# Softplus in one ScalarE function, earlier use of PSUM banks, and sums of states that add to a seeded bank, in a Mamba and attention kernel

## The chip, the cores and the metric

The kernel runs on one core of a Trainium2 chip. The core has five engines with queues of their own: TensorE (PE; PEld is its weight load), VectorE (DVE), ScalarE (ACT), GpSimd (POOL) and SyncE (SP), which here issues nearly all transfers. The metric is the device time of one execution in microseconds (us).

## What is computed

Eight images of 384 channels by 1024 positions go through two layers. The first normalizes, runs a Mamba block forwards and backwards over the 1024 positions, and adds a 3x3 depthwise convolution with a gate. The second is causal attention with six heads, and a feed-forward with binarized weights and quantized activations, which by the reference's grouping works on the first five of the eight images. Cut to what the change touches:

```python
def mamba(x, in_proj_w, conv1d_w, conv1d_b, x_proj_w, dt_proj_w, dt_proj_b, A_log, D_param, out_proj_w):
    ...
    dt, Bm, Cm = jnp.split(x_dbl, [dt_rank, dt_rank + D_STATE], axis=-1)
    delta = jax.nn.softplus(jnp.einsum('blr,dr->bld', dt, dt_proj_w) + dt_proj_b)
    A = -jnp.exp(A_log)
    deltaA = jnp.exp(delta[..., None] * A)
    deltaBu = (delta * u)[..., None] * Bm[:, :, None, :]
    def step(h, inp):
        dA, dBu, c = inp
        h = dA * h + dBu
        return (h, jnp.einsum('bdn,bn->bd', h, c))
    ...
    y = ys.transpose(1, 0, 2) + u * D_param
    y = y * silu(z)
    return jnp.einsum('bld,od->blo', y, out_proj_w)
```

There are 16 states for each of the 384 channels, two directions, and all is float32.

## The kernel before

**Who sets the order.** The program first records every operation (`Plan.record`) with a rank, its place in the order of recording. `Plan.place` then plays the whole kernel through with a cost for each operation, gives every engine the ready operation of lowest rank whose buffers are free, and places its tiles; `Plan.emit` issues all in that order. An engine's queue is therefore fixed when the program is built. `hurry(offset=...)` lowers the rank of what is recorded in it; `together()` makes one operation of several instructions on one engine. All of them reach the profile as line 364, so groups of instructions are told apart by their tiles.

**The scans.** An image has four parts (direction and half of the positions, `PARTS`), three blocks of 128 channels, four groups of states and two halves of channels: 96 units of work, 768 in all. For one unit POOL multiplies delta u by B (`s_first`, two units ahead); ACT makes exp(delta A) in one of two PSUM banks ("da") and DVE scans, twice (`s_scan`, 512 positions each); POOL multiplies by C. There are six buffers for the products (tile `scan_g`). For every second unit `s_sum` sums the states of a pair with four matmuls (tile `ps_y`, one bank); four pairs make one part of one channel block. `s_gate` then closes it: the first direction's y plus D u is kept in `yt`; in the second direction three VectorE steps make y + D u, add yt and multiply by z. `slots` records the scan steps with a rank 600 lower than their place.

**The rest.** `before_scan` prepares an image: norm, input projection, convolutions, u, B, C and delta. `delta` makes softplus for 128 channels and 512 positions from `dp`, a PSUM bank that a matmul with `const_wdt` fills. It takes exp(-|x|), 1 + that, its logarithm, adds max(x, 0) and corrects the rounding of 1 + e: five ScalarE steps and three VectorE steps, before DVE multiplies by u and ACT copies delta to SBUF. Both are stored to DRAM, from where the scans load them spread over partitions. There are 12 such deltas for an image, 96 in all. `attention` is the second layer for one image, `feed_forward` its second half; five PSUM banks ("any") serve all of this. `spread_over` interleaves lists of such steps by their share of their total cost; `before_scan` of images 3 to 7 is interleaved with the feed-forward of images 0 to 4 in this way. Images 0 to 2 are prepared and the weights binarized in an opening stage. At the end `due` times spread the scan slots over the rest, and the attention of the last image's second half runs alone.

ScalarE keeps one table of functions loaded; the kernel stays with the one that has Exp and Ln (`LOG_EXP`), and loads another for Silu, Tanh and Gelu in blocks that end with `preload_act_table_set(LOG_EXP)`.

Of the kernel before, what the change touches and what calls it, by code (L numbers as in the profile page):

```python
# [13 lines left out]
ALU = mybir.AluOpType  # L14
# [146 lines left out]
class Plan:  # L161
# [84 lines left out]
    def place(self):  # L246
# [47 lines left out]
        while events:  # L294
            now = events[0][0]
            while events and events[0][0] <= now:
                heapq.heappop(events)
            moved = True
            while moved:
                moved = False  # L300
                for e in engines:
                    while waiting[e] and waiting[e][0][0] <= now:
                        op = heapq.heappop(waiting[e])[2]
                        if op.start is None:
                            heapq.heappush(ready[e], (op.rank, next(count), op))
                    while free_at[e] <= now and ready[e]:
                        aside, op, held = [], None, set()
                        while ready[e]:
                            item = heapq.heappop(ready[e])
                            if item[2].start is not None:  # L310
                                continue
                            if fits(item[2], now, held):
                                op = item[2]
                                break
                            aside.append(item)
                        for item in aside:
                            heapq.heappush(ready[e], item)
                        if op is None:
                            break
                        op.name, op.start, moved = e, now, True  # L320
                        for t in op.tiles:
                            if t.place is None:
                                k = t.kind
                                k.free.sort()
                                t.place = k.free.pop(0)[1]
                        if op.dma:
                            free_at[e] = now + 0.06
                            dma_free = max(dma_free, now + 1.2) + op.time
                            op.end = dma_free + 1.2
                        else:  # L330
                            op.end = free_at[e] = now + op.time
                        heapq.heappush(events, (free_at[e], next(count), e))
                        done.append(op)
                        for t in op.tiles:
                            users_left[id(t)] -= 1
                            if not users_left[id(t)]:
                                at = max(u.end for u in t.users) + self.SIGNAL
                                t.kind.free.append((at, t.place))
                                t.kind.freed += 1
                                heapq.heappush(events, (at, next(count), e))  # L340
                        for nxt in op.behind:
                            nxt.left -= 1
                            if not nxt.left:
                                release(nxt)
# [33 lines left out]
def kernel(  # L378
# [104 lines left out]
    ident = ctile("ident", [P, P])  # L483
    make_identity(tc.nc, plan.now(ident))

    cmask = ctile("cmask", [P, HB], BF16)
    nc.vector.memset(cmask, 0.0)
    masked = ctile("masked", [P, P])
# [1 line left out]
    nc.vector.tensor_copy(cmask[:, HB - P :], masked)  # L490
    onesc = ctile("onesc", [P, P])
    nc.gpsimd.memset(onesc, 1.0 / C)
    onecol = ctile("onecol", [P, 1])
    nc.gpsimd.memset(onecol, 1.0)
    eps = ctile("eps", [P, 2])
    nc.gpsimd.memset(eps[:, 0:1], 1e-6)
    nc.gpsimd.memset(eps[:, 1:2], 1e-5)
# [141 lines left out]
    def before_scan(b, tags, emit, later=None, diags=None, lead=None):  # L639
# [260 lines left out]

        def delta(c, d, h):
            ew = mtile(f"ew{d}_{b}_{c}_{h}").rearrange("p (i l) -> p i l", i=2)
            du = mtile(f"du{d}_{b}_{c}_{h}").rearrange("p (i l) -> p i l", i=2)
            e, w, dl, u = ew[:, 0, :], ew[:, 1, :], du[:, 0, :], du[:, 1, :]
            load(u, spilled[b, "u", d, c][:, half(h)])
            dp = bank_of(f"dp{d}_{b}_{c}_{h}")
            r = slice(d * DW, d * DW + RANK + 1)
            nc.tensor.matmul(  # L910
                out=dp, lhsT=wdt[r, chunk(c)], rhs=st["xd"][r, half(h)], start=True, stop=True
            )
            nc.scalar.activation(e, dp, AF.Abs)
            nc.scalar.activation(e, e, AF.Exp, scale=-1.0)
            nc.scalar.activation(w, e, AF.Identity, bias=onecol)
            nc.scalar.activation(dl, w, AF.Ln)

            nc.vector.scalar_tensor_tensor(dl, dp, 0.0, dl, ALU.max, ALU.add)
            nc.scalar.copy(dp, w)
            nc.vector.scalar_tensor_tensor(dp, dp, 1.0, e, ALU.subtract, ALU.subtract)  # L920
            nc.vector.tensor_tensor(dp, dl, dp, ALU.subtract)
            nc.vector.tensor_tensor(u, u, dp, ALU.mult)
            nc.scalar.copy(dl, dp)
            for i, what in enumerate(("dl", "ud")):
                t = dram.tile([P, HB], F32, name=f"s{what}_{d}_{b}_{c}_{h}", tag=f"sp_{what}_{d}_{c}_{h}")
                nc.sync.dma_start(out=t, in_=du[:, i, :])
                spilled[b, what, d, c, h] = t

        for d, h in parts_of(b):
            for c in range(NC):  # L930
                to = lead if lead is not None and (d, h) == (0, 0) else emit
                to(lambda c=c, d=d, h=h: delta(c, d, h), 3.0)

# [84 lines left out]
    def s_sum(u):  # L1020

        if u.q == 0:
            sst["pair"] = sst.pop(("g", u.name))
            return
        if u.j == u.first_group:
            sst["y"] = bank(f"y_{u.name}", "y")
        y = sst["y"]
        pair = (sst.pop("pair"), sst.pop(("g", u.name)))
        with together():
            for k in (2, 3, 0, 1):  # L1030
                nc.tensor.matmul(
                    out=y[k * BLK : (k + 1) * BLK, :],
                    lhsT=gather,
                    rhs=pair[k // 2][:, k % 2, :],
                    start=(u.j == u.first_group),
                    stop=(u.j == u.last_group),
                    skip_group_check=True,
                )

    def s_gate(u):  # L1040

        if not u.closes:
            return
        b, c, h, y = u.b, u.c, u.h, sst["y"]
        key = ("yt", b, c, h)
        t = sp.tile([P, HB], F32, name=f"uh_{u.name}", tag="us", bufs=1)
        load(t, spilled[b, "u", u.d, c][:, half(h)])
        if key not in sst:
            yt = sp.tile([P, HB], F32, name=f"yt_{u.name}", tag="yt", bufs=2 * NC)
            with hurry(offset=60):  # L1050
                nc.vector.scalar_tensor_tensor(
                    yt, t, vec[:, c, V_D : V_D + 1], y, ALU.mult, ALU.add
                )
            sst[key] = yt
            return
        z = sp.tile([P, HB], F32, name=f"zh_{u.name}", tag="z", bufs=1)
        load(z, spilled[b, "z", c][:, half(h)])
        yt = sst.pop(key)
        with hurry(offset=60):
            nc.vector.scalar_tensor_tensor(y, t, vec[:, c, V_D : V_D + 1], y, ALU.mult, ALU.add)  # L1060
            nc.vector.tensor_tensor(y, yt, y, ALU.add)
            nc.vector.tensor_tensor(z, z, y, ALU.mult)
        gy = dram.tile([P, HB], F32, name=f"sgy_{u.name}", tag=f"sp_gy_{c}_{h}")
        nc.sync.dma_start(out=gy, in_=z)
        spilled[b, "gy", c, h] = gy
# [424 lines left out]
    class Gap(float):  # L1490
        pass

    def spread_over(*lists):

        keyed = []
        for k, steps in enumerate(lists):
            total, at = sum(us for _, us in steps), 0.0
            for f, us in steps:
                keyed.append(((at + us / 2) / total, k, (f, us)))
                at += us  # L1500
        return [e[2] for e in sorted(keyed, key=lambda e: e[:2])]

# [2 lines left out]
    def slots(lo, hi):  # L1505
# [4 lines left out]
        def slot(k):  # L1510
            at(s_load, k + AHEAD + 2)
            at(lambda u: s_row(u, 0), k + AHEAD + 2)
            at(lambda u: s_row(u, 1), k + 2)
            at(s_first, k + AHEAD)
            at(s_scan, k)
            at(s_sum, k - 1)
            at(s_gate, k - 1)

# [46 lines left out]
    for i, b in enumerate(ORDER):  # L1565
# [2 lines left out]
        fed = Steps()  # L1568
        rest += steps_of(attention, b, fed) if i < B - 1 else []
        if fed and later:  # L1570
            fed = spread_over(fed, steps_of(before_scan, later.pop(0), ("pt", "pt", "av")))
            fed = [(f, JOINT * (SHORT if isinstance(us, Gap) else us)) for f, us in fed]
        rest += fed
        if i == B - 2:
# [73 lines left out]
```

## Time and profile before

| what | us |
|---|---|
| median of three runs | 4101.04 |
| lowest, highest run | 4100.95, 4101.35 |
| the profiled execution's own time | 4101.66 |
| its span, first to last instruction | 4099.8 |
| first product of the scans on POOL starts | 74.7 |
| last one ends | 3921.6 |
| out-projection of image 0 opens on PE | 697.1 |

In the page's table of groups a row names the engine, the operation, the tile written and the tiles read, the shape and the count; then the busy time in us and the mean of one in ns; then the engine's idle time just before such instructions and what ended it. The two groups of POOL are the longest of all:

```profile
L364 POOL TENSOR_TENSOR scan_g<-scan_g,scan_bc 128x1024 f32<-128x1024 f32 x768 | 1814.8, 2368 | 199.3 <-ACT scan_carry L364 116.8
L364 POOL TENSOR_TENSOR scan_g<-scan_ud,scan_bc 128x1024 f32<-128x1024 f32 x768 | 1820.0, 2377 | 140.5 <-DMA scan_ud<-dram_sp_ud 68.4
```

Of the 68.4 us that POOL waited for `scan_ud`, 61.6 are the time before the very first product. The largest DVE groups are the scans themselves, 943.3 and 898.0 us.

### The profile page before, as it was taken

To read this page: it belongs to the slowest core of one execution; us is meant where nothing else is said; L and a number is where in the kernel's file an instruction comes from. 1 tells how busy PE (TensorE), PEld (TensorE's weight loads), DVE (VectorE), ACT (ScalarE), POOL (GpSimd) and SP (SyncE) were. 2 spreads that over 40 slices of the span, in tenths; PEclk is the share of its full clock that TensorE was granted. 3 is DMA by queue.
4 is the path that set the end of the run, shared out by engine and by line. 5 is a ranking of instruction groups with operands and counts; after the bars stand their busy time and mean duration, and the time that the engine had idled before them with its cause. 6 is when DMAs were issued, how large, how long until landed. Compare 5 with 4: busy or idle time off the path is not lost. (4 is left out here: it accounts for less than half of the span.)

```text
span 4099.8 us, 43593 instructions
## 1 busy us (share of the span) xinstructions
PE 3414.5 (83%) x12426; PEld 1336.9 (33%) x12426; DVE 3458.9 (84%) x4867; ACT 2687.2 (66%) x5288; POOL 3577.0 (87%) x1560
## 2 busy tenths in 40 slices
PE   4557387989889898979998798987989879998999
PEld 1112022433323333324333243332433323333344
DVE  5999999888898889988899977999788998877843
ACT  5856767586674867657666667666586665856635
POOL 3999999999799997989998899978899788999920
PEclk8678596999979999889999899997999979999999
DMA  5635655333374344543345633447324464233300
GB/s 195 218 134 189 237 176 209 131 108 133 136 243 146 104 142 146 196 166 115 127 140 174 223 114 115 136 143 268 114 79 133 148 240 169 96 128 110 133 26 31
DMA packets 338971, 612.03 MB, mean 149 GB/s; under 512 B 34617, under 2 KB 93417, under 8 KB 338729
## 3 DMA queue, kind: packets, MB, share of 16 engines
q1 hardware_dynamic: 329072, 593.10, 42.0%
q10 hardware_dynamic: 9656, 16.15, 1.1%
q8 instruction: 98, 1.61, 0.2%
q14 instruction: 145, 1.18, 0.1%
HBM read 456.03 MB, written 153.09 MB: 149 GB/s over the span
## 5 line engine op out<-in xcount | busy, mean ns | idle before, releaser
L364 POOL TENSOR_TENSOR scan_g<-scan_g,scan_bc 128x1024 f32<-128x1024 f32 x768 | 1814.8, 2368 | 199.3 <-ACT scan_carry L364 116.8
L364 POOL TENSOR_TENSOR scan_g<-scan_ud,scan_bc 128x1024 f32<-128x1024 f32 x768 | 1820.0, 2377 | 140.5 <-DMA scan_ud<-dram_sp_ud 68.4
L364 ACT ACTIVATE ps_da<-scan_dl,const_amat 128x512 f32<-128x512 f32 x1536 | 1050.2, 689 | 702.1 <-DVE scan_g L364 688.5
L364 DVE TENSOR_TENSOR_SCAN scan_g<-ps_da,scan_carry,scan_g 128x512 f32<-128x512 f32 x768 | 943.3, 1267 | 99.1 <-POOL scan_g L364 81.2
L364 DVE TENSOR_TENSOR_SCAN scan_g<-ps_da,scan_g 128x512 f32<-128x512 f32 x768 | 898.0, 1208 | 108.4 <-POOL scan_g L364 83.5
L364 PE MATMUL ps_any<-big_big,mid_mid 128*128 128x512 f32 x2016 | 940.9, 619 | 38.5 <-DVE big_big L364 18.4
L364 PE MATMUL ps_y<-scan_g,const_gather 128*32 128x512 f32 x3072 | 477.6, 698 | 299.7 <-POOL scan_g L364 293.9
L364 PEld LDWEIGHTS ps_any<-big_big,mid_mid 128*128 128x128 f32 x2016 | 384.9, 197 | 598.0 <-issue 481.0
L364 PE MATMUL ps_any<-big_big,big_big 128*128 128x512 f32 (+4 forms) x1728 | 558.6, 560 | 22.3 <-ACT ptp_ptn L364 7.4
L364 PE MATMUL ps_any<-const_ident,mid_mid 128*128 128x128 f32 x1728 | 306.7, 306 | 61.9 <-DVE small_nm L364 25.2
L364 DVE CUSTOM_DVE_ANT_0 mid_mid<-ps_any,const_cmask 128x512 f32<-128x512 f32 (+3 forms) x576 | 292.2, 547 | 59.5 <-PE ps_any L364 58.9
L364 PEld LDWEIGHTS ps_any<-big_big,big_big 64*128 64x128 f32 (+1 forms) x1728 | 226.9, 190 | 322.3 <-issue 202.2
L364 DVE SCALAR_TENSOR_TENSOR ps_any<-big_big,const_vec,ps_any 128x496 f32<-128x496 f32 (+6 forms) x420 | 303.2, 727 | 19.1 <-ACT ps_any L364 5.5
L364 PEld LDWEIGHTS ps_any<-const_ident,mid_mid 128*128 128x128 f32 x1728 | 200.1, 150 | 283.8 <-issue 89.1
L364 ACT COPY ptp_ptn<-ps_any 128x512 f32<-128x512 f32 (+3 forms) x576 | 256.2, 478 | 48.9 <-PE ps_any L364 41.1
L364 ACT ACTIVATE mid_mid<-mid_mid,small_low 128x512 f32<-128x512 f32 (+3 forms) x384 | 242.8, 635 | 53.5 <-DVE small_low L364 52.9
L364 PE MATMUL ps_any<-ptp_ptn,big_big 128*64 128x512 f32 (+3 forms) x1152 | 260.6, 532 | 13.1 <-ACT ptp_ptn L364 11.8
L364 PEld LDWEIGHTS ps_y<-scan_g,const_gather 128*32 128x32 f32 x3072 | 64.5, 115 | 595.1 <-POOL scan_g L364 499.4
L364 PE MATMUL ps_any<-mid_mid,const_wdt 25*128 25x512 f32 x192 | 155.3, 939 | 81.5 <-ACT mid_mid L364 51.6
L364 ACT ACTIVATE mid_mid<-mid_mid 128x512 f32<-128x512 f32 (+1 forms) x261 | 188.8, 738 | 3.9
L364 ACT COPY mid_mid<-ps_any 128x512 f32<-128x512 f32 x234 | 134.6, 581 | 79.3 <-DVE mid_mid L364 38.0
L364 PE MATMUL ps_any<-mid_mid,const_onesc 128*128 128x512 f32 x252 | 135.2, 665 | 57.7 <-ACT mid_mid L364 45.3
(106 smaller groups left out, 3467.6 us busy)
## 6 DMA issues: line engine op xcount, KB each, us to landing
scan_ud<-dram_sp_ud SPq DMA_DIRECT2D x384, 256.0 KB, 3.6
scan_dl<-dram_sp_dl SPq DMA_DIRECT2D x384, 256.0 KB, 3.5
scan_bc<-dram_rows SPq DMA_DIRECT2D x256, 256.0 KB, 3.2
scan_us<-dram_sp_u SPq DMA_DIRECT2D x96, 256.0 KB, 2.6
mid_mid<-dram_sp_u SPq DMA_DIRECT2D x96, 256.0 KB, 4.6
dram_sp_ud<-mid_mid SPq DMA_DIRECT2D x96, 256.0 KB, 3.7
dram_sp_dl<-mid_mid SPq DMA_DIRECT2D x96, 256.0 KB, 3.2
dram_sp_u<-mid_mid SPq DMA_DIRECT2D x42, 512.0 KB, 5.1
```

The costliest lines, as they stand in the source:

```text
L364: getattr(engine, what)(*[mapped(v) for v in args], **{k: mapped(v) for k, v in kwargs.items()})
```

## The change

Four edits. `delta` becomes `deltas`: three channel blocks are taken together, each with a PSUM bank; three Softplus run in place in one block with its table loads, and what followed (the product with u, the copy, two stores) stays. The state sums no longer start their bank: `s_skip` loads u some slots ahead, `s_seed` writes D u to the bank (on ScalarE for the first direction), or D u + yt (on DVE, for the second), and all four pairs add to it; a matmul at the start of the program writes the bank once. `s_gate` then only copies y (ScalarE) or multiplies by z (DVE). In the planner an operation of DVE, ACT, POOL or SP that touches a PSUM tile which already has its bank gets a rank lower by 60. And `before_scan` beside a feed-forward has its steps drawn to the first 0.8 of it.

```diff
@@ Plan.place
                         if op.start is None:
-                            heapq.heappush(ready[e], (op.rank, next(count), op))
+                            opened = e != "tensor" and any(
+                                t.place is not None and t.kind.space == PSUM for t in op.tiles
+                            )
+                            heapq.heappush(ready[e], (op.rank - 60 * opened, next(count), op))
@@ constants
+    nc.tensor.matmul(
+        out=bank("written", "y"),
+        lhsT=ident,
+        rhs=wproj.rearrange("p c e -> p (c e)")[:, :HB],
+        start=True,
+        stop=True,
+    )
@@ before_scan
-        def delta(c, d, h):
-            ew = mtile(f"ew{d}_{b}_{c}_{h}").rearrange("p (i l) -> p i l", i=2)
...
-            nc.scalar.activation(e, dp, AF.Abs)
-            nc.scalar.activation(e, e, AF.Exp, scale=-1.0)
-            nc.scalar.activation(w, e, AF.Identity, bias=onecol)
-            nc.scalar.activation(dl, w, AF.Ln)
-
-            nc.vector.scalar_tensor_tensor(dl, dp, 0.0, dl, ALU.max, ALU.add)
-            nc.scalar.copy(dp, w)
-            nc.vector.scalar_tensor_tensor(dp, dp, 1.0, e, ALU.subtract, ALU.subtract)
-            nc.vector.tensor_tensor(dp, dl, dp, ALU.subtract)
-            nc.vector.tensor_tensor(u, u, dp, ALU.mult)
-            nc.scalar.copy(dl, dp)
...
+        def deltas(d, h):
+            st_of = []
+            for c in range(NC):
+                du = mtile(f"du{d}_{b}_{c}_{h}").rearrange("p (i l) -> p i l", i=2)
+                load(du[:, 1, :], spilled[b, "u", d, c][:, half(h)])
+                dp = bank_of(f"dp{d}_{b}_{c}_{h}")
+                r = slice(d * DW, d * DW + RANK + 1)
+                nc.tensor.matmul(
+                    out=dp, lhsT=wdt[r, chunk(c)], rhs=st["xd"][r, half(h)], start=True, stop=True
+                )
+                st_of.append((c, du, dp))
+            with hurry(offset=60), together():
+                for _, _, dp in st_of:
+                    nc.scalar.activation(dp, dp, AF.Softplus)
+                nc.scalar.preload_act_table_set(LOG_EXP)
+            for c, du, dp in st_of:
+                dl, u = du[:, 0, :], du[:, 1, :]
+                nc.vector.tensor_tensor(u, u, dp, ALU.mult)
+                nc.scalar.copy(dl, dp)
...
         for d, h in parts_of(b):
-            for c in range(NC):
-                to = lead if lead is not None and (d, h) == (0, 0) else emit
-                to(lambda c=c, d=d, h=h: delta(c, d, h), 3.0)
+            to = lead if lead is not None and (d, h) == (0, 0) else emit
+            to(lambda d=d, h=h: deltas(d, h), 6.0)
@@ s_sum
-        if u.j == u.first_group:
-            sst["y"] = bank(f"y_{u.name}", "y")
...
-                    start=(u.j == u.first_group),
+                    start=False,
@@
+    def s_skip(u):
...
+        t = sp.tile([P, HB], F32, name=f"uh_{u.name}", tag="us", bufs=2)
+        load(t, spilled[u.b, "u", u.d, u.c][:, half(u.h)])
+        sst["us", u.b, u.c, u.part] = t
+
+    def s_seed(u):
...
+        t, y = sst.pop(("us", u.b, u.c, u.part)), bank(f"y_{u.name}", "y")
+        yt, scale = sst.pop(("yt", u.b, u.c, u.h), None), vec[:, u.c, V_D : V_D + 1]
+        with hurry(offset=60):
+            if yt is None:
+                nc.scalar.activation(y, t, AF.Copy, scale=scale)
+            else:
+                nc.vector.scalar_tensor_tensor(y, t, scale, yt, ALU.mult, ALU.add)
+        sst["y"], sst["second"] = y, yt is not None
@@ s_gate
-                nc.vector.scalar_tensor_tensor(
-                    yt, t, vec[:, c, V_D : V_D + 1], y, ALU.mult, ALU.add
-                )
+                nc.scalar.copy(yt, y)
...
-            nc.vector.scalar_tensor_tensor(y, t, vec[:, c, V_D : V_D + 1], y, ALU.mult, ALU.add)
-            nc.vector.tensor_tensor(y, yt, y, ALU.add)
             nc.vector.tensor_tensor(z, z, y, ALU.mult)
@@ spread_over
-                keyed.append(((at + us / 2) / total, k, (f, us)))
+                share = (at + us / 2) / total
+                keyed.append((share * sooner if k else share, k, (f, us)))
@@ slot
+            at(s_skip, k + 4)
             at(s_scan, k)
+            at(s_seed, k - 1)
             at(s_sum, k - 1)
             at(s_gate, k - 1)
@@
-            fed = spread_over(fed, steps_of(before_scan, later.pop(0), ("pt", "pt", "av")))
+            fed = spread_over(fed, steps_of(before_scan, later.pop(0), ("pt", "pt", "av")), sooner=0.8)
```

More of the change, by code (lines that the diff above doesn't have):

```diff
@@ L492 @@
     nc.gpsimd.memset(onesc, 1.0 / C)
-    onecol = ctile("onecol", [P, 1])
-    nc.gpsimd.memset(onecol, 1.0)
     eps = ctile("eps", [P, 2])
@@ L899, in _ @@
                 spilled[b, "rows", d] = rows
-        def delta(c, d, h):
-            ew = mtile(f"ew{d}_{b}_{c}_{h}").rearrange("p (i l) -> p i l", i=2)
[L905 to L911, printed above, removed]
-            )
-            nc.scalar.activation(e, dp, AF.Abs)
-            nc.scalar.activation(e, e, AF.Exp, scale=-1.0)
-            nc.scalar.activation(w, e, AF.Identity, bias=onecol)
-            nc.scalar.activation(dl, w, AF.Ln)
-            nc.vector.scalar_tensor_tensor(dl, dp, 0.0, dl, ALU.max, ALU.add)
-            nc.scalar.copy(dp, w)
-            nc.vector.scalar_tensor_tensor(dp, dp, 1.0, e, ALU.subtract, ALU.subtract)
-            nc.vector.tensor_tensor(dp, dl, dp, ALU.subtract)
-            nc.vector.tensor_tensor(u, u, dp, ALU.mult)
-            nc.scalar.copy(dl, dp)
[L924 to L927, printed above, removed]
@@ new lines, in deltas @@
+        def deltas(d, h):
[17 more added lines that the diff above has]
+                nc.scalar.copy(dl, dp)
+                for i, what in enumerate(("dl", "ud")):
+                    t = dram.tile(
+                        [P, HB], F32, name=f"s{what}_{d}_{b}_{c}_{h}", tag=f"sp_{what}_{d}_{c}_{h}"
+                    )
+                    nc.sync.dma_start(out=t, in_=du[:, i, :])
+                    spilled[b, what, d, c, h] = t
@@ L1038, in s_sum @@
                 )
+    def s_skip(u):
+        if not u.opens:
+            return
+        t = sp.tile([P, HB], F32, name=f"uh_{u.name}", tag="us", bufs=2)
+        load(t, spilled[u.b, "u", u.d, u.c][:, half(u.h)])
+        sst["us", u.b, u.c, u.part] = t
+    def s_seed(u):
+        if not u.opens:
+            return
+        t, y = sst.pop(("us", u.b, u.c, u.part)), bank(f"y_{u.name}", "y")
[6 more added lines that the diff above has]
+        sst["y"], sst["second"] = y, yt is not None
     def s_gate(u):
@@ L1044, in s_gate @@
         b, c, h, y = u.b, u.c, u.h, sst["y"]
[L1045 to L1048, printed above, removed]
+        if not sst["second"]:
             yt = sp.tile([P, HB], F32, name=f"yt_{u.name}", tag="yt", bufs=2 * NC)
             with hurry(offset=60):
-                nc.vector.scalar_tensor_tensor(
-                    yt, t, vec[:, c, V_D : V_D + 1], y, ALU.mult, ALU.add
-                )
-            sst[key] = yt
+                nc.scalar.copy(yt, y)
+            sst["yt", b, c, h] = yt
             return
@@ L1057, in s_gate @@
         load(z, spilled[b, "z", c][:, half(h)])
-        yt = sst.pop(key)
         with hurry(offset=60):
-            nc.vector.scalar_tensor_tensor(y, t, vec[:, c, V_D : V_D + 1], y, ALU.mult, ALU.add)
-            nc.vector.tensor_tensor(y, yt, y, ALU.add)
             nc.vector.tensor_tensor(z, z, y, ALU.mult)
@@ L1491, with spread_over @@
         pass
-    def spread_over(*lists):
+    def spread_over(*lists, sooner=1.0):
         keyed = []
```

## The prediction

> **What bounds the kernel now.** I read the page's busy shares first, then a table of stretches cut at the POOL instruction that opens each image, then the groups of instructions, then the waits of POOL.
>
> ```profile
> span 4099.8 us, 43593 instructions
> PE 3414.5 (83%) x12426; PEld 1336.9 (33%) x12426; DVE 3458.9 (84%) x4867; ACT 2687.2 (66%) x5288; POOL 3577.0 (87%) x1560
> ```
>
> Three engines stand at 83 to 87%, so the average names no bound. The stretches do (us, then busy time and count of each engine, then the granted TensorE clock):
>
> ```profile
> core 0: us, PE busy (x) PEld busy (x) DVE busy (x) ACT busy (x) POOL busy (x), PEclk, DMA share, GB/s
> 0.00:74.70 74.70, 35.46 (x62) 13.33 (x63) 27.43 (x49) 32.51 (x51) 8.29 (x24) 0.87 0.66 222
> 74.70:540.00 465.30, 255.14 (x709) 73.51 (x711) 434.06 (x522) 317.64 (x540) 444.67 (x193) 0.67 0.56 194
> 540.00:997.00 457.00, 397.84 (x1490) 154.54 (x1483) 393.64 (x559) 315.04 (x641) 444.94 (x192) 0.90 0.43 150
> 997.00:1490.00 493.00, 430.57 (x1567) 170.20 (x1566) 431.91 (x601) 332.80 (x649) 445.82 (x193) 0.91 0.45 152
> 1490.00:1991.00 501.00, 432.02 (x1521) 169.18 (x1520) 443.70 (x621) 334.71 (x646) 447.26 (x193) 0.91 0.44 151
> 1991.00:2483.00 492.00, 433.17 (x1499) 169.86 (x1498) 437.68 (x579) 331.16 (x625) 447.95 (x194) 0.93 0.46 157
> 2483.00:2979.00 496.00, 427.02 (x1464) 166.41 (x1467) 432.23 (x567) 323.27 (x604) 446.25 (x193) 0.92 0.45 155
> 2979.00:3477.00 498.00, 431.54 (x1474) 168.81 (x1468) 436.52 (x572) 325.88 (x607) 447.27 (x193) 0.91 0.44 153
> 3477.00:3921.60 444.60, 403.39 (x1890) 170.49 (x1886) 354.14 (x598) 295.05 (x703) 444.54 (x192) 0.96 0.34 115
> 3921.60:4099.80 178.20, 168.35 (x767) 80.57 (x766) 67.64 (x206) 79.17 (x227) 0.00 (x0) 1.00 0.08 26
> ```
>
> POOL needs 444.6 us for an image's 192 products (2.316 each; 9.27 for a pair of units, four products). Eight images: 3557. The scans take 3921.6 - 74.7 = 3846.9, so 290 us are POOL waiting: 21 and 12 in the first two images, 47 to 56 in each of the five beside which a feed-forward runs, none in the last. The span is 74.7 start + 3557 floor + 290 waits + 178.2 tail. Only the 290, the start and the tail can be won.
>
> In those five images DVE stands at 87 to 89%, the last column but one shows PE at 0.91 of its clock. The worst places are the delta steps (five stretches, from the first to the last small matmul of const_wdt):
>
> ```profile
> 1693.00:1771.00 78.00, 54.38 (x136) 16.66 (x137) 72.34 (x89) 57.40 (x100) 71.07 (x32) 0.68 0.82 283
> ...
> sum 360.00, PE 265.30 PEld 83.97 DVE 328.59 ACT 277.58 POOL 318.88; mean PE 53.06 PEld 16.80 DVE 65.72 ACT 55.52 POOL 63.78
> ```
>
> There DVE is at 91%, PE at 74% with a clock near 0.7, and POOL idles 41 us. The chains of five ScalarE and four VectorE steps per delta are what fills them.
>
> **What the skill says.** "ScalarE: Activation LUTs", section "What ACT_TABLE_LOAD costs": a load of 1283 ns plus a drain of about 1380, 2.66 us a switch. The trace agrees with the first (1283) and not the second: the median gap on ACT after a load is 11 ns, before it 18. I use 1.28. The same page ("Step-by-step") says that every function runs at one element per cycle and lane, so Softplus should cost what another function does; the row for 512 elements in PSUM without an operand for the bias has 578 ns. "PSUM — Partial Sum Buffer", section "The four PSUM rules": ScalarE and VectorE writes leave the written bits alone, and a matmul without the first flag adds where the bit is set; hence the dummy matmul at the start. No trace of before shows such a sum. "Trainium Kernel Development and Optimization", "Performance Expectations", calls matmul busy time a bad measure of nearness to the limit; here stretches with PE at 97% of the time and POOL at 100% exist (3600 to 3700), so 90% isn't yet a wall.
>
> **The change part by part.**
>
> ```profile
> L364 DVE SCALAR_TENSOR_TENSOR mid_mid<-ps_any,mid_mid 128x512 f32<-128x512 f32 x126 | 83.3, 677 | 14.4 <-ACT mid_mid L364 14.2
> L364 DVE SCALAR_TENSOR_TENSOR ps_any<-ps_any,mid_mid 128x512 f32<-128x512 f32 x96 | 65.4, 681 | 8.4 <-ACT ps_any L364 7.8
> L364 DVE TENSOR_TENSOR ps_any<-mid_mid,ps_any 128x512 f32<-128x512 f32 x96 | 66.6, 694 | 2.9
> L364 DVE SCALAR_TENSOR_TENSOR scan_yt<-scan_us,const_vec,ps_y 128x512 f32<-128x512 f32 x48 | 35.5, 739 | 29.5 <-PE ps_y L364 29.5
> L364 DVE TENSOR_TENSOR ps_y<-scan_yt,ps_y 128x512 f32<-128x512 f32 x48 | 33.4, 696 | 1.7
> L364 ACT ACT_TABLE_LOAD x67 | 86.0, 1283 | 1.8 <-PEq L1635 0.7
> ```
>
> *Softplus.* Per delta DVE loses 0.677 + 0.681 + 0.694 = 2.05 us, 197 over 96. ACT loses Abs 0.59, Exp 0.63, Identity 0.72, Ln 0.63 and the copy back to PSUM 0.58, 3.15 us, 302 in all; it gains 96 x 0.58 = 56 and 32 blocks x 2 loads x 1.28 = 82. Net ACT -164. The multiply by u and the copy of delta stay. A block holds ACT for 2.57 + 1.74 = 4.3 us. Queued behind it are the Exps of the scans (two banks) and the evictions for which PE waits. POOL's second product of a unit comes four products (9.3 us) after the first, of which the scan needs about 3, so 4.3 us is covered; today's Gelu block (four of 2.85 us and loads, 14 us) isn't, and the largest POOL waits stand beside it: 9 to 16 us each, 57 in the five images. These stay.
>
> *The sums.* DVE loses 35.5 + 33.4 = 69 us: the first direction's sum with D u and the addition of yt. The second direction's D u, 36.0 us, becomes the seed. ACT gains 48 seeds at 0.69 and 48 copies at 0.58, 61 us. A bank then passes from last matmul to copy to seed to next matmul, about 1.3 us and two signals where one or three DVE steps stood (0.74 or 2.1 us). The next sums come a pair later, 9.3 us, so it is covered unless ACT is in a long block; PE waits for yt and z in all of before 4.5 us. The load of u is only issued some units earlier.
>
> *Sooner.* Steps on an already open bank move up 60 ranks, and the scan preparation is drawn into the first 80% of the feed-forward. Nothing is added or removed. Bounds: -20 us (PE gets banks earlier) to +20 (the 48 VectorE sums of an image's local convolution crowd together); I take 0.
>
> *Start.* The small matmul chain ends as now (three extra ScalarE copies stand in the way of its last sum, +0.8 us), and the deltas finish some 7 us earlier than 70.5. But in the changed SP queue three stores of the second half's u, which wait for a Silu block behind the Softplus block, stand ahead of the first loads of ud. By adding up that queue (Softplus done about 61, copies 63, Silu 67, stores, eight loads at 0.6, landing 3.6) POOL starts near 75.5: +1, bounds -6 to +4. The dummy matmul waits for wproj, landing at 22.2, before the second sum of squares, which starts at 23.6 anyway: nothing.
>
> *What it is worth.* In the instruction order of both programs I counted on PE how many pairs are summed before an image's out-projection opens. Before: 63, 116, 170, 221, 274, 326, 352, 379 of 384. After: 51, 109, 167, 221, 273, 324, 352, 380. So the opening stage is done 12 pairs sooner and the rest is spread over more pairs, with the same end: the tail stays.
> Opening stage: today 622.3 us (74.7 to 697) for 63 pairs, 38 over its floor, DVE busy 573.4. After: minus 36 x 2.05 = 74, minus 12 gates x 0.72 = 9, minus 12 pairs of scans at 4.95 = 59, gives 431 over a floor of 51 x 9.27 = 473. That is 91%, as today (92%), so the same share of waits: 29 us.
> From there to image 7's out-projection: today 3190 us for 316 pairs, floor 2929, 261 over, DVE busy 2765 (87%). After: 329 pairs, floor 3050; DVE 2765 - 123 (60 deltas) - 59 (82 gates) + 64 (13 pairs) = 2647, again 87% if nothing waits. PE has 2804 today at 88%; a clock of 0.9 in place of 0.7 in the delta stretches saves 60, 2744 over 3050 is 90%. So average room exists at the floor, and local waits remain: the Gelu blocks' 57, and I take 45 more for PE's queue and crowded convolutions. Both are estimates.
> Sum: 75.7 + 3557 + 29 + 102 + 178.2 = 3942. What lies outside the span is 4101.66 - 4099.8 = 1.9 in the profiled execution, whose time is 0.6 above the median: 1.3. **Forecast 3943 us**, 158 less.
>
> **Rivals.**
> *Larger.* All waits but the Gelu blocks' go: 75.7 + 3557 + 57 + 178.2 + 1.3 = 3869. For it: the last image has DVE at 80% and no wait at all. Against: PE would need 90% and more.
> *Smaller.* PE is the bound beside the feed-forward; only the 41 us of idle POOL in the delta stretches and 15 of the opening go: 4045. For it: PE is at 88% and the windows 3400 to 3700 reach 96%. Against: the low clock in the delta stretches.
> *Slower.* A block needs three of the five shared banks at once: from the first matmul to the last copy 2.8 + 1.28 + 1.74 + 1.28 + 2.1 = 9.2 us. If PE stands still for part of it, each lost us costs 32. It eats the gain of 158 from 4.9 us a block on; at 7 us: 224 - 158 = +66, 4167. Against: today three chains in flight hold as many banks, and a second-layer sum fills one bank for 24 passes, so two free banks feed PE.
> *No change* would need a Softplus of several passes or loads of 2.66 us (88 more on ACT, which stands at 66%) and full PE; it is small.
>
> **How the numbers follow.** Forecast 0.60 (spread 3880 to 4020 from waits of 65 to 205 us), larger 0.17, smaller 0.12, no change 0.03, slower 0.08. About 0.2% (8 us) is what can be told from no change here. The range takes in larger and smaller: 3860 to 4050. Faster 0.89, same 0.03, slower 0.08.
>
> **What would show it.** Softplus rows of about 0.58 us x96; some 64 more table loads of 1.28; DVE near 3190 busy, ACT near 2585; POOL still about 3570, starting at 75, its waits near 130 and those by the Gelu still there; out-projection of image 0 opening near 575; delta stretches with PE's clock over 0.85; tail of 178. I am wrong if POOL waits rise behind the sums in PE's queue, if PE idles for ACT through the Softplus blocks, or if PE passes 93% with POOL still waiting.

## The result, and the profile after

The changed kernel takes 4127.99 us (median of four, 4124.73 to 4134.4) against 4101.19 for the one before: a ratio of 1.0066, 95% interval 1.0049 to 1.0084. It is slower by 27 us where 158 less were forecast, and outside the range. The profiled execution took 4134.4 us.

The page's first lines after:

```profile
span 4132.5 us, 42977 instructions
## 1 busy us (share of the span) xinstructions
PE 3427.8 (83%) x12428; PEld 1347.4 (33%) x12428; DVE 3343.9 (81%) x4479; ACT 2599.0 (63%) x5068; POOL 3587.5 (87%) x1559
```

DVE has 388 instructions fewer, about as it should (three for each of 96 deltas, two for each of 48 pairs of gates, 384 in all; the planner also gave four copies to ACT that DVE had before), but its busy time fell by 115 us and not by 266. ACT has 2599 (2585 forecast). So 150 us of DVE time came from somewhere. The table of stretches, cut at the first product of each image as before (us, then busy time and count of PE, its weight loads, DVE, ACT and POOL, then PE's granted clock, the DMA share and GB/s; the last row is the tail):

```profile
76.90:553.00 476.10, 316.90 (x859) 104.10 (x860) 427.39 (x485) 309.76 (x505) 445.19 (x192) 0.74 0.59 203
553.00:1024.00 471.00, 401.98 (x1500) 157.94 (x1502) 397.41 (x527) 313.96 (x627) 445.64 (x193) 0.90 0.43 144
1024.00:1498.00 474.00, 385.57 (x1460) 153.06 (x1460) 390.23 (x508) 295.72 (x590) 448.47 (x193) 0.88 0.43 146
1498.00:1981.00 483.00, 400.69 (x1448) 154.64 (x1446) 413.10 (x541) 310.57 (x594) 450.50 (x194) 0.90 0.45 152
1981.00:2485.00 504.00, 436.33 (x1492) 171.12 (x1494) 414.38 (x531) 318.59 (x595) 447.91 (x193) 0.91 0.46 156
2485.00:2982.00 497.00, 433.20 (x1496) 170.10 (x1494) 412.68 (x529) 316.86 (x588) 448.02 (x193) 0.91 0.46 156
2982.00:3481.00 499.00, 436.25 (x1494) 169.57 (x1490) 410.04 (x529) 314.03 (x580) 447.93 (x192) 0.91 0.46 154
3481.00:3945.60 464.60, 398.81 (x1838) 167.69 (x1834) 376.27 (x575) 299.02 (x707) 445.57 (x192) 0.92 0.32 106
3945.60:4132.50 186.90, 176.37 (x788) 83.84 (x784) 67.92 (x207) 79.28 (x227) 0.00 (x0) 1.00 0.07 25
```

Against POOL's 444.6 an image, the waits are now 31, 26, 29, 38, 59, 52, 54 and 20 us: 312 in place of 290. Of the five images with a feed-forward beside them two gained 18 or 19 us, one lost 12 and two are as before; but the images that had almost no waits, the second (12) and the last (none), now have 26 and 20. So something new costs time also where no feed-forward runs beside the scans.

The group of the second direction's seed names it. The first row is the second direction's D u in the kernel before, the row from which the seed was priced; the other three are of the changed kernel:

```profile
L364 DVE SCALAR_TENSOR_TENSOR ps_y<-scan_us,const_vec,ps_y 128x512 f32<-128x512 f32 x48 | 36.0, 750 | 30.0 <-PE ps_y L364 30.0
...
L367 DVE SCALAR_TENSOR_TENSOR ps_y<-scan_us,const_vec,scan_yt 128x512 f32<-128x512 f32 x48 | 178.9, 3726 | 3.9 <-ACT scan_yt L367 3.5
L367 ACT ACTIVATE ps_any<-ps_any 128x512 f32<-128x512 f32 x138 | 75.1, 580 | 8.9 <-PE ps_any L367 7.2
L367 ACT ACT_TABLE_LOAD x131 | 168.1, 1283 | 3.0 <-PEq L1658 0.7
```

The seed takes 3726 ns, five times the 0.75 us at which it was counted: 143 us too many over 48 seeds, nearly all of the missing DVE time. It is not waiting for a semaphore (DVE idled 3.9 us before all 48 together); it is long after it has begun. The same operation before read u from SBUF and y from PSUM and had 750 ns. The new one reads u and `yt`, both from SBUF. The other two rows are Softplus (96 of the 138 in a group whose mean is 580 ns, as forecast) and the table loads (64 more at 1283 ns).

A timeline at one of the six seeds of image 0 (start, duration, engine, operation):

```profile
436.93 6.94 POOL L367 TENSOR_TENSOR scan_g<-scan_ud,scan_bc 128x1024 f32<-128x1024 f32 x3
437.21 7.22 DVE L367 SCALAR_TENSOR_TENSOR ps_y<-scan_us,const_vec,scan_yt 128x512 f32<-128x512 f32 x1
...
444.35 0.73 DVE L367 SCALAR_TENSOR_TENSOR big_big<-big_big,const_vec,ps_any 128x512 f32<-128x512 f32 x1
...
445.14 3.78 PE L367 MATMUL ps_any<-big_big,mid_mid 128*128 128x512 f32 x4 [5.81 <-DVE big_big L367]
...
447.02 1.25 DVE L367 TENSOR_TENSOR_SCAN scan_g<-ps_da,scan_carry,scan_g 128x512 f32<-128x512 f32 x1
```

The seed begins 0.3 us after three back-to-back products on POOL have begun, and ends 0.56 us after the last of them (443.87 to 444.43). Behind it in DVE's queue stood a norm for which PE idled 5.81 us, and a scan for which POOL then waited. Of the 48 seeds 41 took more than 1.2 us, and every one of these ended between 553 and 561 ns after the end of some product on POOL: the instruction stands still until a product ends and is done 0.56 us later.

In 24 of the 41 POOL had a pause after that product, as here. In the other 17 the next product had already begun, and now it was POOL's turn to stand still: that product took 2.8 us, against a median of 2.36 over all. One of these, by the lines of POOL and of DVE (the two views are put together here):

```profile
1433.13 2.36 POOL L367 TENSOR_TENSOR scan_g<-scan_g,scan_bc 128x1024 f32<-128x1024 f32 x1
1435.45 2.81 POOL L367 TENSOR_TENSOR scan_g<-scan_ud,scan_bc 128x1024 f32<-128x1024 f32 x1
...
1433.44 2.61 DVE L367 SCALAR_TENSOR_TENSOR ps_y<-scan_us,const_vec,scan_yt 128x512 f32<-128x512 f32 x1
```

### The profile page after: what moved, and what is told of

It is laid out like the page before. It is cut to its first block, busy times and chain, and to the rows that moved or that the text cites. A ratio compares the mean times of both kernels' runs of the same rounds, so it can differ in the third digit from the quotient of the medians.

```text
span 4132.5 us, 42977 instructions
## 1 busy us (share of the span) xinstructions
PE 3427.8 (83%) x12428; PEld 1347.4 (33%) x12428; DVE 3343.9 (81%) x4479; ACT 2599.0 (63%) x5068; POOL 3587.5 (87%) x1559
## 5 line engine op out<-in xcount | busy, mean ns | idle before, releaser
L367 PE MATMUL ps_any<-big_big,mid_mid 128*128 128x512 f32 x2016 | 975.0, 637 | 91.4 <-DVE big_big L367 62.7
L367 PE MATMUL ps_y<-scan_g,const_gather 128*32 128x512 f32 x3072 | 463.0, 678 | 226.0 <-POOL scan_g L367 205.9
L367 PEld LDWEIGHTS ps_any<-big_big,mid_mid 128*128 128x128 f32 x2016 | 396.5, 203 | 692.9 <-issue 501.2
L367 DVE SCALAR_TENSOR_TENSOR ps_y<-scan_us,const_vec,scan_yt 128x512 f32<-128x512 f32 x48 | 178.9, 3726 | 3.9 <-ACT scan_yt L367 3.5
L367 ACT ACT_TABLE_LOAD x131 | 168.1, 1283 | 3.0 <-PEq L1658 0.7
```

The costliest lines, as they stand in the source:

```text
L367: getattr(engine, what)(*[mapped(v) for v in args], **{k: mapped(v) for k, v in kwargs.items()})
```

## The experiments

Each is compared with the kernel before; the ratios have intervals of 0.1 to 0.2% to either side.

**The seed split.**

```diff
-            if yt is None:
-                nc.scalar.activation(y, t, AF.Copy, scale=scale)
-            else:
-                nc.vector.scalar_tensor_tensor(y, t, scale, yt, ALU.mult, ALU.add)
+            nc.scalar.activation(y, t, AF.Copy, scale=scale)
+            if yt is not None:
+                nc.vector.tensor_tensor(y, yt, y, ALU.add)
```

> After, but the second direction's seed is made in two steps, each with one tensor in SBUF and one in PSUM: ScalarE writes D u to the bank, VectorE adds yt to the bank in place. Theory P (the seed that reads two SBUF tensors waits for POOL's products to pause, 48 x about 3 us of DVE): no DVE row of ps_y has a mean over 0.8 us, and most of what the prediction missed comes back: 3950 to 4040 us. Theory Q (PE's and ACT's order, the blocks of three): within 15 us of after, 4113 to 4143.

Measured 3991.31 us, ratio 0.9731 (0.9716 to 0.9745): 137 us faster than after, 110 faster than before, the fastest of the complete kernels run here. That is in theory P's range. The VectorE sum has 681 ns:

```profile
L367 DVE TENSOR_TENSOR ps_y<-scan_yt,ps_y 128x512 f32<-128x512 f32 x48 | 32.7, 681 | 4.8 <-ACT ps_y L367 4.8
```

The kernel's stretches of images 1, 2, 5 and 7 (counted from 0), and the tail:

```profile
537.00:987.00 450.00, 394.70 (x1494) 155.69 (x1494) 377.47 (x528) 317.50 (x635) 445.12 (x194) 0.91 0.45 150
987.00:1446.00 459.00, 395.52 (x1495) 155.82 (x1488) 369.75 (x518) 306.69 (x606) 447.94 (x193) 0.90 0.46 155
...
2391.00:2876.00 485.00, 425.45 (x1484) 166.82 (x1482) 398.91 (x523) 319.69 (x590) 445.90 (x194) 0.93 0.47 160
...
3361.00:3806.10 445.10, 392.17 (x1846) 164.08 (x1842) 344.37 (x578) 303.09 (x712) 444.69 (x192) 0.95 0.33 111
3806.10:3989.70 183.60, 173.04 (x778) 82.41 (x776) 66.91 (x206) 79.28 (x227) 0.04 (x1) 1.00 0.07 25
```

Image 1 is within 6 us of POOL's floor of 444.6 again, and image 7 is at it. Some 12 to 26 us are gone from every image.

**Softplus alone**, `deltas` in the kernel before and nothing else.

> Before with the blocks of three Softplus alone: gates, ranks and the mix with the feed-forward as before. Theory P: this part is sound and takes DVE 197 us and ACT 164 us of work away: 4000 to 4060 us. Theory Q (a block holds ACT and three of five banks): no faster than before, 4100 to 4180.

4049.6 us, 0.9872 (0.9857 to 0.9887): -52, in theory P's range. If the blocks of three do harm, it is less than what they save; that settles the slower rival of the prediction: three of five banks in one block isn't what made the kernel slower. But DVE's busy time fell by 176 us (3283.1 in place of 3458.9), and that gave only 52.

**The seeds alone**, as the change made them, in the kernel before.

> Before with the seeded banks alone, delta as before. Theory P: slower than before by the seeds' waits, 48 x 3 = 144 us of DVE less the 69 us that it saves, and products on POOL held off: 4120 to 4220 us, the seed on DVE with a mean of 3 us or more. Theory Q: within 25 us of before, 4076 to 4126.

4188.22 us, 1.0207 (1.0190 to 1.0224): +86, as theory P had it, with a seed of 3285 ns:

```profile
L364 DVE SCALAR_TENSOR_TENSOR ps_y<-scan_us,const_vec,scan_yt 128x512 f32<-128x512 f32 x48 | 157.7, 3285 | 4.8 <-ACT scan_yt L364 4.4
```

**After without the seeds**: gates and sums of before; Softplus, ranks and mix stay.

> After with the sums and gates of before: Softplus in blocks, ranks lower by 60 for open banks, and the preparation in the first 0.8 of the feed-forward. Theory P: as fast as the split seed within 20 us, 3960 to 4050. Theory Q: 4100 to 4150.

4044.41 us, 0.9858 (0.9843 to 0.9873). That lies in the range given (3960 to 4050), but is 53 us slower than the split seed, where 20 were allowed: once repaired, the seeds are worth something beside Softplus, the ranks and the mix.

**One operand.** For the second direction ScalarE copies `yt` to the bank, then VectorE adds D u. In the two runs the instructions on every engine come in the same order; one operand of 48 instructions differs. (The first line below is in both runs, the minus is the first run, the plus the second.)

```diff
+                nc.scalar.copy(y, yt)
-                nc.vector.scalar_tensor_tensor(y, t, scale, yt, ALU.mult, ALU.add)   # both in SBUF
+                nc.vector.scalar_tensor_tensor(y, t, scale, y, ALU.mult, ALU.add)    # y in PSUM
```

> The queues of all five engines are the same as in the next run, and one operand differs: ScalarE first copies yt to the bank, then VectorE writes D u + yt to it and reads both u and yt from SBUF. Theory P (two SBUF operands wait for POOL to pause): the 48 rows have a mean of 3 us or more as in after, and the time is near after's 4128: 4090 to 4150 us. Theory R (what made after slow was the place of the seeds in the order): the same time as the next run within 10 us.

> As the run before, but VectorE reads yt from the bank to which ScalarE copied it, and u from SBUF. Theory P: the 48 rows at 0.75 us, and 3980 to 4010 us as with the split seed. Theory R: within 10 us of the run before, wherever that is.

4120.34 us (4115.2 to 4131.07) and 4010.22 us (4009.29 to 4012.05). The two groups:

```profile
L367 DVE SCALAR_TENSOR_TENSOR ps_y<-scan_us,const_vec,scan_yt 128x512 f32<-128x512 f32 x48 | 171.1, 3565 | 10.3 <-ACT ps_y L367 10.3
```

```profile
L367 DVE SCALAR_TENSOR_TENSOR ps_y<-scan_us,const_vec,ps_y 128x512 f32<-128x512 f32 x48 | 35.5, 739 | 10.3 <-ACT ps_y L367 10.2
```

With the order fixed, one operand in SBUF instead of PSUM costs 110 us; DVE's busy time in these rows differs by 135.6. With y in PSUM none of the 48 took over 756 ns, whatever POOL did. The place of the seeds in the queues can't be what separates the two. POOL's waits (whom for, us in total, times, longest) of the first and the second run:

```profile
POOL scan_g L367 <- ACT scan_carry L367: 102.9, 58, 7.1
POOL scan_g L367 <- DVE scan_g L367: 90.4, 43, 11.9
```

```profile
POOL scan_g L367 <- ACT scan_carry L367: 55.9, 34, 6.5
POOL scan_g L367 <- DVE scan_g L367: 50.1, 25, 11.9
```

Both rows end at a scan: the carry is copied from it. These two make up 87 us of the difference, and POOL's own busy time is 12 us longer in the first run (3587.8 and 3576.1), since there the seeds hold up products in their turn. POOL holds up the seed, the seed the scans, and they POOL.

**The ranks and the mix, each left out of the split seed**; then both.

```diff
-                            heapq.heappush(ready[e], (op.rank - 60 * opened, next(count), op))
+                            heapq.heappush(ready[e], (op.rank - 0 * opened, next(count), op))
```

```diff
-            fed = spread_over(fed, steps_of(before_scan, later.pop(0), ("pt", "pt", "av")), sooner=0.8)
+            fed = spread_over(fed, steps_of(before_scan, later.pop(0), ("pt", "pt", "av")), sooner=1.0)
```

> Split seed without the lower rank of operations on open banks. If the ranks are worth nothing, as the prediction took them: 3975 to 4010 us. If earlier free banks feed PE in the stretches where it is the bound: slower than the split seed by 15 to 60.

> Split seed with the scan preparation spread over the whole feed-forward as before. If this edit is worth nothing, as predicted: 3975 to 4010 us. If the crowding of the preparation in the first 0.8 is what still holds up POOL in images 4 to 6 (40 us of waits each): faster, 3940 to 3975. If the free last fifth is what helps: slower by 15 to 40.

> Softplus blocks and split seeds alone: ranks and the mix with the feed-forward as before. Leaving out one of the two cost 43 and 39 us. If they act separately: 4060 to 4085 us. If each needs the other: 4025 to 4050.

4034.15, 4029.89 and 4025.76 us. Without both the kernel is 34 us slower than the split seed, and with only one of them it is slower still by 8 or 4: beside Softplus and the split seeds the two edits are worth 34 us together and nothing one by one. With the gates of before, both together gave 5 (4049.6 to 4044.41). Where most of the time goes can be seen in POOL's waits for the sums (`ps_y`): 47 us with both, 85, 95 and 89 in the three runs; the row of the run without the mix:

```profile
POOL scan_g L367 <- PE ps_y L367: 95.5, 18, 25.1
```

Its longest single wait is 25.1 us, against 10.2 with both. Why each edit needs the other was not settled.

**The split seeds alone**, in the kernel before.

> Before with the seeded banks alone, the second seed split into a ScalarE write and a VectorE sum in the bank. Theory P: 100 to 150 us faster than the seeds alone as the change made them (4188): 4040 to 4090 us. If the seeds were harmful for another reason too: above 4110.

4113.64 us, 1.0024 (1.0015 to 1.0033): 75 us faster than with the two SBUF operands, not the 100 to 150 expected, and even slower than before by 10. That lies above the 4110 from which the seeds were said to do harm for another reason too; which one wasn't found. Less work on DVE (busy 3394.9 in place of 3458.9) and 80 us more on ACT was no gain at all. What the repaired seeds are worth thus depends on what stands beside them: a loss of 10 us alone, a gain of 24 beside Softplus (4049.6 to 4025.76) and of 53 beside all the rest (4044.41 to 3991.31).

**The clip left out.** The minima after Gelu read one tensor in SBUF and write SBUF. In the kernel before, 12 of the 20 take about 1.75 us, the others up to 3.9:

```profile
L364 DVE TENSOR_SCALAR big_big<-big_big 128x3072 f32<-128x3072 f32 x20 | 45.9, 2326 | 6.8 <-ACT big_big L364 6.8
```

Each of the eight long ones ended 1616 to 1621 ns after the end of a product on POOL. So the trace of before already held instructions that stand still for POOL, though none that reads two tensors.

```diff
-                for q in range(NF // NC):
-                    nc.vector.tensor_scalar(st["h", q], st["h", q], QCLIP, None, ALU.min)
```

> Split seed, and the 20 VectorE minima that clip the feed-forward's hidden layer after Gelu are left out (so values just above 127.99999 are not cut). They have one SBUF operand and run at 1.75 us where POOL pauses and up to 4.9 us where it works. If they wait for POOL as the seed did and hold up the scans at the end of the Gelu block: 15 to 45 us faster than the split seed, 3945 to 3977 us, and POOL's waits beside Gelu at half or less. If they lie beside ScalarE's block anyway: within 10 us, 3981 to 4001.

3981.51 us: 10 less than the split seed, at the edge of the second case's range. POOL still idles about as long beside the Gelu blocks (45 us in place of 42, from 5 us before each block to 20 after), so it is not the clip that holds up the scans there. ScalarE's block is what is left; no run here takes it away.

**yt added at the gate** and not before the sums, otherwise as the split seed:

```diff
+            nc.vector.tensor_tensor(y, sst["second"], y, ALU.add)
             nc.vector.tensor_tensor(z, z, y, ALU.mult)
```

> Split seed, but yt is added to the bank at the gate and not before the sums: same instructions, the bank is ready for the sums a step earlier and is given up a step later. Within 15 us of the split seed, 3976 to 4006; slower if the bank's release is what POOL waits for (47 us of POOL's waits were for the sums).

4006.92 us: 16 slower than the split seed, or 12 by the two ratios to before (0.9761 and 0.9731), where 15 were allowed. POOL's waits for the sums stay (48.8 for 47.1 us), so the bank's release isn't shown as the cause.

## Why the prediction was wrong

**The step that failed** is in *The sums*: "The second direction's D u, 36.0 us, becomes the seed." Its price was read from a row of the same operation, shape and output, with y in PSUM. In the new instruction y's place is taken by `yt`, in SBUF, and POOL is busy 87% of the time. It measured 3726 ns. The Trainium skill states the ground for it: "GPSIMD Engine Reference", section "Specifications", says that GpSimd's SBUF interfaces are shared with VectorE, with contention for VectorE instructions that have two SBUF inputs. The section gives no size; the traces agree, and give one: 39 to 41 of 48 such seeds stood still until a product ended, and one operand was worth 110 us. The prediction mentions neither the operands' places nor that page. The row of 750 ns was no bound for the seed, and no other row could be one: in the trace of before no VectorE instruction of this size reads two tensors from SBUF. The edit got no bounds and no rival. In 4128 - 3943 = 185 us of error this step is 137 (after against the split seed), or 110 by the pair with the same order; in the kernel before, without the other edits, it was 75.

**The remaining 48 us** are sizes. The split seed, with a DVE busy time near the forecast (3198.5, forecast 3190), ran 3991. By the prediction's own sum: start 76.2 (75.7 forecast), tail 183.6 (178.2), waits 3806.1 - 76.2 - 3557 = 173 (131). So nearly all of it is in the waits. They stand in images 4 to 6, 40 to 43 us each, and are 5 to 16 in images 0 to 3. The opening stage had 28 us (29 forecast), so the term of 102 for the Gelu blocks, PE's queue and crowded convolutions was too small by about 42. The trace puts 47 us of POOL's waits down to the sums on PE and 96 to scans and their carries, some 37 of these beside the Gelu blocks; for all but the Gelu blocks' the prediction had taken 45. What held them up in images 4 to 6 was not settled. PE's busy share is 87 to 88% there, and the same in images 1 and 7, which hardly wait, so that share is no sign of it.

*Softplus* was right in mechanism and price: 580 ns, loads of 1283. The five delta stretches shrank from 360 to 185 us after the change, in the view by windows:

```profile
sum 185.00, PE 164.29 PEld 54.91 DVE 120.89 ACT 145.54 POOL 171.40; mean PE 32.86 PEld 10.98 DVE 24.18 ACT 29.11 POOL 34.28
```

POOL is busy for 171 of these 185 us, so the blocks on ACT hardly hold it up. The clock there is 0.68 to 0.79, not over 0.85 as forecast, so the 60 us of PE time that a clock of 0.9 was to save are not to be had in full: PE's busy time fell by 35 us in all with the split seed (3414.5 to 3379.5). What the edit brings alone, 52 us, is a quarter of the 197 us of DVE time that it was to save.

*Sooner* was taken as 0 within 20 us to either side: with the sums repaired it is a gain of 34, and the ranks and the mix only work together.

*Start* was right: the first product starts at 76.9 (75.7, within its bounds), and in SP's queue the three stores of u stand ahead of the first loads, as read there. The *opening* was done at 602 us and not at 575 (586 with the seed split). The Gelu blocks' waits did not stay whole: POOL idled 67 us beside them before, 38 after and 42 with the split seed (from 5 us before each block to 20 after).

**Of the rivals**, the slower one named the wrong place: Softplus alone, with its blocks of three banks, is faster. That the kernel came out slower, as this rival said, is luck: it did so by another mechanism.

## What to carry to other kernels

Before pricing an instruction from a row of the same operation, compare where each operand lies: moving one from PSUM to SBUF took this one from 0.74 to 3.6 us while POOL was busy. A group whose instructions of one shape differ much in length, without a wait on a semaphore before them, is a sign to look at what another engine does meanwhile; the clip was such a group before the change. The remedy here was cheap, one operand through PSUM (ScalarE writes, VectorE adds in place), and the sum of four edits turned from +27 to -110 us. A measured loss of a bundle says little on its parts: one part of four did most of the harm here, and two were worth nothing without each other.

## What the runs showed of the hardware

A VectorE operation of 128x512 float32 with both tensors in SBUF doesn't share with POOL's products (about 2.35 us each, two SBUF inputs); it stands still until one of them ends. In three kernels (after, the seeds alone, and the first of the pair) 39 to 41 of 48 such instructions took over 1.2 us, and each ended 553 to 562 ns after a product's end. The others took 0.73 to 1.2 us; all but one of them had begun in the last part of a product. Of the 121 long ones about half, 61, got in where POOL paused; the other 60 got in although the next product had begun, and that product then took about 2.8 us. So each of the two engines can hold up the other. To have begun first is not enough: a waiting seed was passed over by up to five products in a row, the longest wait being 12.1 us. What decides at which product's end it gets in was not found.

A VectorE minimum of 128x3072 float32 with one tensor, SBUF to SBUF, does the same: in the kernel before 8 of 20 took 1.9 to 3.9 us instead of 1.75 and ended 1616 to 1621 ns after a product's end.
